# Queries less each head's maximum: two VectorE operations, or two ScalarE multiplications and a GpSimd addition

## The chip, the core and the metric

The kernel runs on one core of one Trainium2 chip. A core has five engines that each work through a queue of instructions in order: TensorE (PE; PEld is its weight load) for matrix products and transpositions, VectorE (DVE), ScalarE (ACT) and GpSimd (POOL) for elementwise work, and SyncE (SP), which issues transfers here. Tiles lie in the on-chip memory SBUF, matmul results in the banks of PSUM. The metric is the device time of one execution in microseconds.

## What is computed

Two decoder layers over x of 16 sequences x 128 tokens x 256 features, each with three blocks. Layer 0 has causal single-head attention, cross attention with 16 heads of 16 features over a context, and a feed-forward network of 16 blocks of 64 of which a router picks four. Layer 1 has self-attention with 16 heads, attention over the context with rotated queries and keys and a mask by position and by cell number, and a mixture of eight experts (two chosen) and two shared ones.

The change lies in the 16-head attention, which three of the six blocks use. For one sequence and each head it is

```python
scores = jnp.einsum('bqhd,bkhd->bhqk', qh, kh) / np.sqrt(D_HEAD)
scores = jnp.where(attention_mask[:, None, :, :], NEG_FILL, scores)
probs = jax.nn.softmax(scores, axis=-1)
out = jnp.einsum('bhqk,bkhd->bqhd', probs, vh)
```

with 1/sqrt(256) and no mask in layer 1's self-attention. A softmax is unchanged when each row's maximum is taken off before the exponential.

## The kernel before, in words

**Order of the work.** The 16 sequences make eight pairs (G = 2). Each pair goes through a layer as a chain of steps written as a Python generator. `Turns` (line 74 on) is a planner that runs while the program is built: it holds up to five such chains at a time, keeps an estimated free time for every engine, and each time resumes the chain that could go on soonest, which then records its next instructions. A step names its engine and the buffers that it takes (`yield DVE, dict(qs=1)`), and `q.give` returns them. The estimates are 150 + 1.05 ns a column for VectorE, 220 + 0.8 for ScalarE, 60 + 1.7 or (two tensors) 60 + 2.5 for GpSimd, and 150 ns for a change of engine. So the order on every engine's queue comes from these estimates, and it is fixed once the program is built. The experts of layer 1 start as further chains when the last pair has left layer 0 and their weights have been asked for (`late_weights`: the two gu loads and down, 3 MB), at most three at a time.

All engines' instructions are recorded by helpers, so that the profile has one line for each: 113 matmuls, 117 transpositions, 121 VectorE, 125 ScalarE, 131 GpSimd. The names of the tiles tell them apart.

**The attention of one sequence** (`attention`, line 471) runs twice over the scores. The 16 heads are two chunks (DC) of eight, and the eight are four rows of 32 features with two heads each (HR). `spread` has made from the keys kT the tile kb, in which, for each of two heads, the other head's features are zeroed and one of them is set to one. The first pass (s<-kb,qT, with the mask added by a product with the identity, s<-ident,unseen) gives the scores with the queries on the partitions; VectorE reduces them to the negative maximum of each query and head (top), which frees the score banks. TensorE transposes top (topT, in a bank). VectorE adds to the queries qT, for each of the two heads, the transposed maxima times a 0/1 column (`heads`) that puts them on the features of the one head's place: this is qs. The second pass (s<-qs,kb) then gives scores less the maximum with the keys on the partitions. Where there is a mask, VectorE adds it (p<-s,unseen); ScalarE takes the exponential; TensorE multiplies with the values (oT), which have a column of ones for the sum, ScalarE copies (oS), TensorE transposes (o), and VectorE divides.

**Buffers** (`LIMITS`, line 332): four general PSUM banks, two score tiles that each pass takes both of (`s=2`), three qs, three top, three tmp. The tmp buffers hold the experts' tanh (sg) and, in the windowed attention, the comparison of cells.

**Around it.** GpSimd computes normalise's reciprocal root in four small operations (rstd, less), spreads the keys (kb, four operations a pair), adds residuals and biases, and rotates queries and keys (qT<-qT,consts, then qT<-qT,swap): the swap tile is made by two DMAs that SP issues, and VectorE multiplies it by the sines between the two. SP's queue holds these, the loads of ctx, of masks and cells, the late weights, and the stores, in one order.

Of the kernel before, what the change touches and what calls it, by code (L numbers as in the profile page):

```python
# [14 lines left out]
ALU = mybir.AluOpType  # L15
AX = mybir.AxisListType

B, S, D = 16, 128, 256
P = 128
DC = D // P  # L20
# [8 lines left out]
HR = RT // HD  # L29
# [41 lines left out]
PE, DVE, ACT, POOL, SP = "PE", "DVE", "ACT", "POOL", "SP"  # L71
# [149 lines left out]
def decoder(ctx: ExitStack, tc: tile.TileContext, a: dict, out: bass.AP):  # L221
# [9 lines left out]
    def bank(shape, name):  # L231
        return ps.tile(shape, F32, tag="bank", name=name)
# [52 lines left out]
    heads = consts[:, C_HEADS : C_HEADS + HR]  # L285
# [8 lines left out]
    def along(t, n):  # L294

        return t.unsqueeze(2).to_broadcast([t.shape[0], t.shape[1], n])
# [30 lines left out]
    for name, scale in (("L0_xattn_bq", 0.25), ("L1_attn_b_q", 0.0625), ("L1_xattn_b_q", 0.25)):  # L327
        t = scaled_bias[name] = keep.tile([P, DC], F32, name=f"scaled_{name}")
# [4 lines left out]
        bank=4, s=2, oT=1, xn=6, xT=5, qk=5, qs=3, kb=4, v=4, p=4, oS=2, on=4, hm=8, tmp=3, rank=2, selT=2, p0=2,  # L333
        pT0=2, unseen=4, cell=2, chosen=3, swap=2, words=2, top=3,
    )
    q = Turns(nc, LIMITS)

    def new(tag, shape, name, dtype=F32):
        return work.tile(shape, dtype, tag=tag, name=name, bufs=LIMITS[tag])
# [127 lines left out]
    def banks():  # L467

        return [ps_s.tile([P, 2, HR, DC, S], F32, tag="s", name="s") for _ in range(2)]

    def attention(qT, kb, v, j, unseen=None, to=None):

        js = slice(j * S, (j + 1) * S)
        yield PE, dict(s=2)
        ss = banks()
        if unseen is not None:  # L480
            for r in range(4):
                q.matmul(
                    ss[r // 2][:, r % 2].rearrange("p h e s -> p (h e) s"), unseen,
                    ident16.unsqueeze(1).to_broadcast([P, HR * DC, S]), start=True, stop=False,
                )
        for e in range(DC):
            for r in range(4):
                at = slice(r * RT, (r + 1) * RT)
                q.matmul(
                    ss[r // 2][:, r % 2, :, e], qT[at, e, js], kb[at, e, :, js],  # L490
                    start=unseen is None, stop=unseen is None or e == DC - 1,
                )
        yield DVE, dict(top=1)
        top = tops.pop(0)
        for t2, s in enumerate(ss):
            q.dve(
                "tensor_reduce", top[:, t2 * 2 * RT : (t2 + 1) * 2 * RT].rearrange("p (h d) -> p h d", d=HD)[:, :, 0:DC],
                s.rearrange("p r h e s -> p (r h) e s"), AX.X, ALU.max, negate=True,
            )
            q.give("s")  # L500
        yield PE, dict(bank=1)
        t = bank([P, S], "topT")
        q.transpose(t, top, ident)
        q.give("top")
        tops.append(top)
        yield DVE, dict(qs=1)
        qs = new("qs", [P, DC, HR, S], "qs")
        for h in range(HR):
            q.dve(
                "scalar_tensor_tensor",  # L510
                qs[:, :, h, :], t.unsqueeze(1).to_broadcast([P, DC, S]), heads[:, h : h + 1], qT[:, :, js],
                ALU.mult, ALU.add,
            )
        q.give("bank")
        yield PE, dict(s=2)
        ss = banks()
        for e in range(DC):
            for h in range(HR):
                for r in range(4):
                    at = slice(r * RT, (r + 1) * RT)  # L520
                    q.matmul(
                        ss[r // 2][:, r % 2, h, e], kb[at, e, h, js], qs[at, e, h, :], start=True, stop=True
                    )
        q.give("qs")

        def exponentials(s):
            s = s.rearrange("p r h e s -> p (r h e) s")
            if unseen is None:
                yield ACT, dict(p=1)
                p = new("p", [P, HC, S], "p")  # L530
                q.act("activation", p, s, AF.Exp)
                q.give("s")
            else:
                yield DVE, dict(p=1)
                p = new("p", [P, HC, S], "p")
                q.dve("tensor_tensor", p, s, unseen.unsqueeze(1).to_broadcast([P, HC, S]), ALU.add)
                q.give("s")
                yield ACT
                q.act("activation", p, p, AF.Exp)
            return p  # L540

        pTs = yield [exponentials(s) for s in ss]
        yield PE, dict(oT=1, bank=1)

        oT = bank([P, H // 4, S], "oT")
        for t2 in range(2):
            for e in range(DC):
                for n in range(2):
                    for i in range(HR):
                        h = e * HC + (2 * t2 + n) * HR + i  # L550
                        c4 = h % 4
                        q.matmul(
                            oT[c4 * CT : (c4 + 1) * CT, h // 4, :],
                            v[:, j, h * HA : h * HA + CT], pTs[t2][:, (n * HR + 1 - i) * DC + e, :],
                            start=True, stop=True,
                        )
        q.give("p", 2)
        yield ACT, dict(oS=1)
        oS = new("oS", [P, H // 4, S], "oS")
        q.act("copy", oS, oT)  # L560
        q.give("oT")
        q.give("bank")
        yield PE, dict(bank=1)
        o = bank([P, H // 4, S], "o")
        for t4 in range(H // 4):
            q.transpose(o[:, t4, :], oS[:, t4, :], ident)
        q.give("oS")
        yield DVE, dict(on=1) if to is None else {}
        o = o.rearrange("p t (c a) -> p (t c) a", a=CT)
        r = small.tile([P, H], F32, tag="r", name="r")  # L570
        q.dve("reciprocal", r, o[:, :, HD])
        if to is None:
            to = new("on", [P, D], "on")
        q.dve("tensor_tensor", to.rearrange("p (h e) -> p h e", e=HD), o[:, :, 0:HD], along(r, HD), ALU.mult)
        q.give("bank")
        return to
# [144 lines left out]
    def context_attention(l):  # L721
# [23 lines left out]
        def one(j):  # L745
            yield POOL, dict(unseen=1)
            unseen = new("unseen", [P, S], "unseen", BF16)
            q.pool("tensor_scalar", unseen, mask[:, j, :], OUT, 1.0, ALU.mult, ALU.mult)
            on = yield from attention(qT, kb, v, j, unseen=unseen)
            q.give("unseen")  # L750
            yield POOL
            q.pool("tensor_tensor", x[l][:, j, :], x[l][:, j, :], on, ALU.add)
            q.give("on")
# [66 lines left out]
    def self_attention(l):  # L820
# [24 lines left out]
        def one(j):  # L845
            on = yield from attention(qT, kb, v, j)
            yield from output_projection(on, w["o1"], l, j, free="on")
# [7 lines left out]
    def windowed_attention(l):  # L855
# [33 lines left out]
        def one(j):  # L889
            b = l * G + j  # L890
            yield DVE, dict(unseen=1, tmp=1)

            other = new("tmp", [P, S], "other")
            q.dve(
                "tensor_scalar",
                other, cell_k[:, j * S : (j + 1) * S], cell_q[:, b : b + 1], -1.0, ALU.is_equal, ALU.add
            )
            unseen = new("unseen", [P, S], "unseen4", BF16)
            q.dve("scalar_tensor_tensor", unseen, other, -OUT, causal_T, ALU.mult, ALU.min)
            q.give("tmp")  # L900
            yield from attention(qT, kb, v, j, unseen=unseen, to=on[:, j, :])
            q.give("unseen")
            yield POOL
            q.pool("tensor_tensor", x[l][:, j, :], x[l][:, j, :], row("L1_xattn_b_o"), ALU.add)
# [230 lines left out]
```

## Time and profile before

| | |
|---|---|
| median of 3 runs (range) | 894.0 us (891.85 to 896.6) |
| the profiled execution | 889.73 us |
| its span, first to last instruction | 887.9 us |
| mean granted TensorE clock | 0.981 |
| instructions | 17836 |
| queries with maxima (qs, VectorE) | 96 operations, 451 to 485 ns |
| maxima (top, VectorE) | 96 operations, 1191 to 1225 ns |
| first and last attention's maxima start at | 53.6 and 725.2 us |

The profile shows one execution. The busy time of an engine is the time in which it executes something. A wait is put down to the instruction that ended last before the waiting one started. The chain of waits goes back from the last instruction, at each step to what released it. A group line names output and inputs, shape and count, and then busy time and the mean duration of one; the figure behind the bar is the engine's idle time in front of these instructions. In the chain, pieces of one kind that follow each other are merged, and their count stands behind the x.

### The profile page before, as it was taken

How to read it: one execution, taken by the hardware profiler on the slowest of the kernel's cores; microseconds unless marked ns; L12 is line 12 of the kernel's file. 1: busy time of each engine (PE TensorE's matmuls, PEld its weight loads, DVE VectorE, ACT ScalarE, POOL GpSimd, SP SyncE). 2: the span in 40 equal slices, each digit the busy share in tenths (PEclk: the TensorE clock that was granted, in tenths of full speed). 3: DMA queues.
4: the chain of work that ended last, by engine and by line, in shares of the span. 5: the costliest groups of instructions: out<-in, count | busy, mean ns of one | idle time of the engine just before them, and what ended most of it. 6: DMA issues, size and time to landing. Idle time of an engine off the chain costs nothing.

```text
span 887.9 us, 17836 instructions
## 1 busy us (share of the span) xinstructions
PE 834.6 (94%) x7232; PEld 671.9 (76%) x7232; DVE 578.5 (65%) x1378; ACT 348.0 (39%) x705; POOL 286.7 (32%) x558
## 2 busy tenths in 40 slices
PE   3999999999999999999798989979998999999998
PEld 2867778778777777877666857758786878888887
DVE  4358866456458476278588969676887686556443
ACT  2435443453435253444534625434633323122111
POOL 4023534124334225273762742405251402000000
PEclk9999999999999999999998989989997999999999
DMA  9400000000000000231000100101010000000000
GB/s 341 154 3 15 3 1 13 2 16 13 3 1 14 1 2 1 70 116 44 18 25 1 43 1 1 43 18 38 13 32 13 30 1 13 13 1 13 12 13 13
DMA packets 16961, 25.94 MB, mean 29 GB/s; under 512 B 3184, under 2 KB 12400, under 8 KB 16240
## 3 DMA queue, kind: packets, MB, share of 16 engines
q1 hardware_dynamic: 16880, 24.81, 8.2%
q8 instruction: 57, 0.93, 0.4%
q14 instruction: 24, 0.20, 0.1%
HBM read 18.51 MB, written 2.10 MB: 23 GB/s over the span
## 4 chain that ended last, share of the span: by engine, by line
PE 78%; DVE 11%; POOL 5%; ACT 3%; DMA 2%; issue 2%; SPq 0%; POOLq 0%; ACTq 0%; DVEq 0%
PE gu L113 15%; PE y L113 14%; PE s L113 12%; PE pj L113 9%; PE pr L113 7%; PE hp L113 7%; PE oT L113 4%; PE tps L117 2%; DVE top L121 2%; PE o L117 2%; DVE st L121 1%; POOL rstd L131 1%; PE rt L113 1%; DVE qs L121 1%; POOL kb L131 1%
## 5 line engine op out<-in xcount | busy, mean ns | idle before, releaser
L121 DVE TENSOR_REDUCE top<-s 128x8 f32<-128x1024 f32 x96 | 112.7, 1216 | 30.7 <-PE s L113 30.4
L113 PE MATMUL gu<-srcT,gu 128*128 128x256 f32 x512 | 117.7, 381 | 0.7 <-ACT oT L125 0.3
L113 PEld LDWEIGHTS gu<-srcT,gu 128*128 128x128 f32 x512 | 94.7, 190 | 14.6 <-ACT oT L125 0.6
L131 POOL TENSOR_SCALAR rstd<-mv 128x2 f32<-128x2 f32 x72 | 16.8, 233 | 236.1 <-DVE mv L121 203.2
L121 DVE TENSOR_TENSOR p<-s,unseen 128x1024 f32<-128x1024 f32 x64 | 76.0, 1217 | 21.0 <-PE s L113 21.0
L125 ACT ACTIVATE sg<-gu 128x256 f32<-128x256 f32 x80 | 30.6, 383 | 135.8 <-PE gu L113 134.3
L125 ACT ACTIVATE p<-p 128x1024 f32<-128x1024 f32 x64 | 66.8, 1059 | 35.8 <-DVE p L121 35.3
L113 PE MATMUL s<-qs,kb 32*128 32x128 f32 x1536 | 61.8, 293 | 8.6 <-DVE top L121 7.3
L113 PEld LDWEIGHTS s<-qs,kb 32*128 32x128 f32 x1536 | 51.4, 194 | 22.2 <-issue 10.7
L113 PE MATMUL hp<-srcT,L_w 128*128 128x256 f32 x256 | 66.0, 387 | 0.0
L131 POOL TENSOR_TENSOR eq<-eq,consts 128x512 f32<-128x512 f32 (+1 forms) x16 | 14.7, 916 | 157.2 <-DVE eq L121 157.2
L113 PE MATMUL y<-L_w,hm 128*128 128x256 f32 x256 | 58.9, 383 | 0.0
L113 PE MATMUL y<-down,hm 128*128 128x256 f32 x256 | 58.6, 382 | 0.0
L113 PE MATMUL s<-kb,qT 32*128 32x256 f32 x768 | 56.5, 406 | 0.0
L131 POOL TENSOR_SCALAR kb<-kT,consts 128x256 f32<-128x256 f32 x96 | 52.7, 562 | 11.7 <-ACT kT L125 10.9
L121 DVE TENSOR_TENSOR x<-x,y 128x256 f32<-128x256 f32 x32 | 13.4, 420 | 64.9 <-PE y L113 64.9
L113 PEld LDWEIGHTS hp<-srcT,L_w 128*128 128x128 f32 x256 | 44.3, 190 | 12.3 <-issue 2.4
L131 POOL TENSOR_TENSOR rstd<-rstd,power 128x2 f32<-128x2 f32 x72 | 51.7, 717 | 6.0
L121 DVE SCALAR_TENSOR_TENSOR sg<-sg,gu 128x256 f32<-128x256 f32 x80 | 33.3, 416 | 31.2 <-ACT sg L125 31.1
L113 PEld LDWEIGHTS y<-L_w,hm 128*128 128x128 f32 x256 | 47.6, 190 | 7.9 <-issue 1.1
L113 PE MATMUL oT<-p,v 128*32 128x128 f32 x1536 | 52.8, 277 | 0.4 <-ACT p L125 0.3
L113 PEld LDWEIGHTS y<-down,hm 128*128 128x128 f32 x256 | 47.7, 190 | 6.8 <-DVE hm L121 0.4
(150 smaller groups left out, 1671.7 us busy)
## 6 DMA issues: line engine op xcount, KB each, us to landing
c<-in_ctx SPq DMA_DIRECT2D x16, 256.0 KB, 2.9
x<-in_x SPq DMA_DIRECT2D x8, 256.0 KB, 6.0
L_w<-in_L_w SPq DMA_DIRECT2D x2, 1024.0 KB, 8.6
swap<-qT SPq DMA_DIRECT2D x16, 128.0 KB, 2.0
swap<-kT SPq DMA_DIRECT2D x16, 128.0 KB, 2.1
gu<-in_L_gu SPq DMA_DIRECT2D x2, 1024.0 KB, 5.0
out_x<-x SPq DMA_DIRECT2D x8, 256.0 KB, 2.1
down<-in_L_down SPq DMA_DIRECT2D x1, 1024.0 KB, 7.0
```

The source lines that it names most:

```text
L113: self.nc.tensor.matmul(out, lhsT, rhs, **kw)
L117: self.nc.tensor.transpose(out, src, ident)
L121: getattr(self.nc.vector, name)(out, *args, **kw)
L125: getattr(self.nc.scalar, name)(out, *args, **kw)
L131: getattr(self.nc.gpsimd, name)(out, *args, **kw)
```

## The change

The two VectorE operations become three of other engines. ScalarE multiplies the transposed maxima by each of the two 0/1 columns into a new tile `less` of 128x256, which is taken from the tmp buffers, and then returns the bank. GpSimd adds `less`, repeated over the two chunks, to the queries, repeated over the two heads, in one operation of 512 columns.[...]

```diff
         q.transpose(t, top, ident)
         q.give("top")
         tops.append(top)
-        yield DVE, dict(qs=1)
+        yield ACT, dict(tmp=1)
+        less = new("tmp", [P, HR, S], "less")
+        for h in range(HR):
+            q.act("mul", less[:, h, :], t, heads[:, h : h + 1])
+        q.give("bank")
+        yield POOL, dict(qs=1)
         qs = new("qs", [P, DC, HR, S], "qs")
-        for h in range(HR):
-            q.dve(
-                "scalar_tensor_tensor",
-                qs[:, :, h, :], t.unsqueeze(1).to_broadcast([P, DC, S]), heads[:, h : h + 1], qT[:, :, js],
-                ALU.mult, ALU.add,
-            )
-        q.give("bank")
+        shape = [P, DC, HR, S]
+        q.pool(
+            "tensor_tensor", qs, qT[:, :, js].unsqueeze(2).to_broadcast(shape), less.unsqueeze(1).to_broadcast(shape), ALU.add
+        )
+        q.give("tmp")
         yield PE, dict(s=2)
```

No other line differs, but the planner works with the new steps and their estimates, so the order of nearly everything after the first attention is another one, on every queue.

## Prediction

> **What bounds the kernel now.** I read the page first, then a table of the span in stretches, the waits, the chain of waits in time, and the instruction orders of both built kernels.
>
> The page: busy times, and the chain that ended last by engine and by line.
>
> ```profile
> PE 834.6 (94%) x7232; PEld 671.9 (76%) x7232; DVE 578.5 (65%) x1378; ACT 348.0 (39%) x705; POOL 286.7 (32%) x558
> ...
> PE 78%; DVE 11%; POOL 5%; ACT 3%; DMA 2%; issue 2%; SPq 0%; POOLq 0%; ACTq 0%; DVEq 0%
> PE gu L113 15%; PE y L113 14%; PE s L113 12%; PE pj L113 9%; PE pr L113 7%; PE hp L113 7%; PE oT L113 4%; PE tps L117 2%; DVE top L121 2%; PE o L117 2%; DVE st L121 1%; POOL rstd L131 1%; PE rt L113 1%; DVE qs L121 1%; POOL kb L131 1%
> ```
>
> TensorE is the bound, and the change takes no work from it. Only TensorE's idle time, 887.9 - 834.6 = 53.3 us, and what the others do to it, can move.
>
> The stretches (columns: stretch, length, then busy us of PE, PEld, DVE, ACT, POOL, then the granted clock):
>
> ```profile
> 0.00:60.00 60.00, 44.55 (x247) 36.59 (x247) 23.83 (x78) 22.56 (x58) 18.08 (x52) 1.00 0.52 184
> 60.00:120.00 60.00, 56.81 (x636) 44.31 (x636) 48.26 (x104) 28.96 (x58) 22.98 (x45) 1.00 0.03 7
> 440.00:540.00 100.00, 89.30 (x983) 68.38 (x981) 82.00 (x187) 45.65 (x85) 50.19 (x93) 0.93 0.06 20
> 540.00:640.00 100.00, 93.54 (x1009) 73.37 (x1005) 75.37 (x162) 47.67 (x88) 31.45 (x61) 0.97 0.07 25
> 740.00:888.00 148.00, 143.97 (x740) 124.30 (x732) 78.67 (x240) 26.71 (x70) 10.32 (x26) 1.00 0.03 11
> ```
>
> 60 - 44.6 = 15.4 us of the idle time is the start, and 4.0 us the last stretch, in which no attention runs. The other 34 us lie between 60 and 740 us, where all 48 attentions are. Where TensorE idles most (440 to 540), VectorE is 82% busy and the clock is below 1.
>
> The waits between 60 and 740 us (sum us, times, longest):
>
> ```profile
> PE s L113 <- DVE top L121: 7.3, 5, 3.2
> PE topT L117 <- DVE qs L121: 6.0, 3, 3.1
> ...
> PE tps L117 <- DVE qs L121: 2.5, 1, 2.5
> ```
>
> The groups by shape (count, busy us, mean ns):
>
> ```profile
> L121 DVE SCALAR_TENSOR_TENSOR qs<-topT,consts,qT 128x256 f32<-128x256 f32 x96 | 41.7, 476 | 14.7 <-PE topT L117 13.7 <-PE s L113 0.7
> ...
> L131 POOL TENSOR_TENSOR eq<-eq,consts 128x512 f32<-128x512 f32 x8 | 11.4, 1422 | 63.2 <-DVE eq L121 63.2
> ...
> L131 POOL TENSOR_TENSOR kT<-kT,consts 128x512 f32<-128x512 f32 x8 | 10.2, 1269 | 0.0
> ...
> L125 ACT COPY pT<-pt 128x128 f32<-128x128 f32 x16 | 3.9, 274 | 10.9 <-PE pt L117 10.8
> ```
>
> The chain through the longest stall (start, us):
>
> ```profile
> 466.28 0.78 DVE qs L121 x2
> 467.07 2.26 DVE top L121 x2
> ...
> 472.53 0.76 DVE qs L121 x2
> 473.29 2.27 DVE top L121 x2
> 475.57 0.14 issue
> 475.70 2.08 PE s L113 x28
> ```
>
> Here the queries stand in VectorE's queue ahead of the maxima (top) that free the score banks; TensorE waits for the maxima, not for the queries.
>
> **What the Trainium skill says.** "Perfetto Trace Analysis", Identifying the Most-Contended Engine: matmul busy time flatters TensorE, weight-load busy time is the better measure. It agrees: weight loads are busy 124.3 of 148 us (84%) in the last stretch but 68% from 440 to 540. "ScalarE: Activation LUTs", What ACT_TABLE_LOAD costs: 186 ns + 0.833 ns a column, and some 93 ns for each pointer operand. The trace agrees on the pointer: the 128x256 copies out of PSUM (oT, v) take 375 ns, the biased hm 471. "GPSIMD Engine Reference", 3.1: a two-input operation costs about 2.6 cycles an element at 1.2 GHz, by estimate 1.1 us for 512; the trace's 1.27 to 1.42 us decide. "SBUF — State Buffer", Who interferes with whom: a VectorE instruction with two SBUF inputs and a GpSimd instruction that reads SBUF lock each other out; one with a single SBUF input does not. The trace fits: the 512-column swap product, two SBUF inputs, has a minimum of 672 ns, a mean of 888 and a maximum of 1646, while top and p, which read PSUM, keep to 1191 to 1226.
>
> **The change part by part.** Removed: 96 VectorE operations, 41.7 us. On the chain the pair appears eleven times, summed piece by piece 8.9 us (the page's 1%), nearly always as something in front of another operation. In two of these (578.7 and 674.5 us) TensorE waits right behind the pair; ScalarE then stands there for 0.74 us instead, so they gain almost nothing, and at 402.6 the maximum is late next anyway. That leaves 8.9 - 0.77 - 0.79 - 0.79 = 6.6 us; I take -6.6, between 0 and -8.9 for the pieces alone. The bound of a full relief is higher: of TensorE's waits 7.3 + 6.0 + 2.5 us name top and qs, and unseen, p and v another 5.8, together 21.6 us.
>
> Added on ScalarE: 96 multiplications of 128x128 out of PSUM with a pointer scale. The plain copy takes 274 ns, the pointer 471 - 375 = 96: 370 ns, 35.5 us in all. By the skill's figures it is 186 + 107 + 93 = 386. ScalarE goes from 348 to 384 us (43%); behind the multiplication in its queue stand exponentials (1.06 us), which feed TensorE's oT, but ScalarE idles over half of every stretch after 60 us. Cost nothing; if that cover fails, 0.74 us at a place.
>
> Added on GpSimd: 48 additions of 512 columns. Nearest rows 1269 and 1422 ns: I take 1.35 us, 65 us in all, GpSimd from 287 to 352 us. Both operands are broadcast over four dimensions, which no row shows; if each took twice that, 2.7 us, it would be 130.
>
> Latency: a pair took 0.95 us from the transposition (2 x 476 ns); now 0.74 + 1.35 us and one more hop between engines (some 0.1 us a hop on the chain): 2.3 us, with waiting room 2.6. I took from the two built orders how much TensorE work stands between each topT and its score matmuls, each matmul at the trace's spacing (0.43 us for 128x256, 1.17 for 16 of s<-qs, 1.08 for 16 of oT). Before, one of 48 lies under 1.35 us and the shortage sums to 1.1 us; after, four lie under 2.6 us, shortage 3.5. Cost +2.4; ends 0 and +9 (the sum at 3.5 us, 8.7).
>
> GpSimd's queue: the addition stands behind everything there. Three kinds of instruction matter: the rotation, whose first product waits for the swap DMA (12.5 and 19.0 us were its two waits before, harmless then); the spreading of keys, four of 0.56 us behind ScalarE's kT; and normalise's four, 1.4 us. In the stretches 414 to 427 and 500 to 515 us GpSimd alone carries the chain, 27 us. Attentions come at 6 in 80 and 9 in 100 us there, 0.08 a us, so 2.2 additions of 1.35 us fall into these stretches: +3.0; ends 0 and +10, the upper end where one addition is held behind a late swap for the 7.2 us that the ctx load took behind the late weights at 383 us. In the changed order SP issues the two gu and the down load ahead of the first query swap instead of behind it; that swap then shares the DMA queue with 3 MB. Its GpSimd product has one key addition in front and six instructions before the next query addition, whose scores come 6 us after their transposition: I put it at nothing, 5 us if the cover is gone.
>
> The order: the builder picks the next step by its estimated costs, so all queues move. The score banks are taken by every score pass and are freed some 2.6 us after it (two maxima or two sums of 1.22 us and hops). Summed over the orders, the TensorE work between one pass and the next falls short of 2.6 us by 16.9 us before and 21.5 after: +4.6; ends -5 and +12. The worst cluster before (6.2 us short) is the 460 to 480 us stall, where PE idled 5.8, so the measure has some hold. After, the worst is 8.5 and a second one has 5.8. The first expert matmul, the filler, has 2603 matmuls in front of it instead of 2505; the attention's end moves little (412 instead of 434 left behind it).
>
> The clock: from 420 to 700 us it was below 1 in eight 20 us slices, worth 17 us, in or just behind the slices with idle time; 17 / 34 is half a us for each us of idle. Sum: -6.6 + 2.4 + 3.0 + 4.6 = +3.4, times 1.5 = **+5.1 us**. The profiled execution, span 887.9, took 889.7 us in all: 894.8. It ran 4.3 us below the median of the runs, so on the median **899.1**.
>
> **Rivals.** *VectorE's relief decides* (the other side): of the 21.6 us of waits on VectorE between 60 and 740 us a third goes, 7.2 us, as VectorE falls from some 80% to 74% busy in the crowded stretches, and clock with it, x1.5: -10.8, so 883. It decides from the point where the new additions find GpSimd free, so that the latency and queue terms (5.4 us) vanish. For it: in the long stalls the chain is solid VectorE. Against: the orders show more crowding of the score banks. *Covered*: relief and new waits cancel, 894, for TensorE is full in half the slices. *GpSimd becomes the bound*: additions at 2.7 us, or held behind rotations; another 48 x 1.35 = 65 us on GpSimd, of which a quarter shows, 16: 915. *It doesn't do what it says* is excluded: in the built order VectorE has 96 operations less, ScalarE 96 and GpSimd 48 more.
>
> **How the numbers follow.** A change under 0.5% (4.5 us) can't be told from none here. Slightly slower, my forecast: 0.38, 899, own range 896 to 907. GpSimd the bound: 0.12. Covered: 0.17. Relief: 0.33. Of the forecast's 0.38 some 0.06 lie within the bound, and 0.02 of the covered case lie above it: slower 0.46, same 0.21, faster 0.33. The range leaves out half of the GpSimd case and the lower third of the relief case: 880 to 912.
>
> **What would show it.** VectorE's busy time down by about 42 us, ScalarE's up by 34 to 37, GpSimd's by 61 to 68. qs additions at 1.3 to 1.45 us. TensorE's waits naming GpSimd's qs in sum 3 to 10 us, and POOL above 5% on the chain. Idle time between 60 and 740 us at 36 to 40 instead of 34 us. Wrong if that idle time falls under 30 us, or if the additions take over 2 us.

## Result: faster by 0.9%

| | kernel before | kernel after |
|---|---|---|
| median (range), 6 runs each | 893.36 us (890.36 to 896.6) | 884.63 us (883.16 to 887.65) |
| ratio, 95% interval | | 0.9907 (0.9879 to 0.9936) |
| the profiled execution | 889.73 us | 883.19 us |
| its span | 887.9 us | 881.4 us |
| mean granted clock | 0.981 | 0.988 |

The gain is clear of noise, 8.3 us by the ratio. The forecast was 899, slower. The time lies within the stated range of 880 to 912, but on the other side of the kernel before, 1.6 us above the 883 of the rival "VectorE's relief decides".

### The profile after

The page of the kernel after: busy times, then the chain that ended last by engine and by line.

```profile
PE 833.8 (95%) x7232; PEld 669.4 (76%) x7232; DVE 546.8 (62%) x1282; ACT 376.4 (43%) x801; POOL 346.4 (39%) x606
...
PE 80%; DVE 8%; POOL 6%; ACT 3%; issue 2%; DMA 1%; SPq 0%; POOLq 0%; DVEq 0%; ACTq 0%
PE gu L113 15%; PE y L113 14%; PE s L113 13%; PE pj L113 10%; PE pr L113 8%; PE hp L113 7%; PE oT L113 5%; PE tps L117 2%; PE o L117 2%; DVE p L121 2%; DVE top L121 1%; POOL rstd L131 1%; POOL kb L131 1%; PE rt L113 1%; DVE st L121 1%
```

TensorE's work is the same and its idle time falls from 53.3 to 881.4 - 833.8 = 47.6 us. VectorE's share of the chain falls from 11 to 8%, qs leaves the list, and GpSimd gains only one point.

Stretches of the span (stretch, length, then busy us of PE, PEld, DVE, ACT, POOL, then the clock). The one with all the attentions, in the kernel before:

```profile
60.00:740.00 680.00, 646.08 (x6253) 510.96 (x6257) 475.98 (x1062) 298.74 (x577) 258.32 (x480) 0.97 0.06 19
```

And in the kernel after, with the start, the crowded stretch and the end:

```profile
0.00:60.00 60.00, 44.57 (x246) 36.91 (x247) 23.21 (x77) 23.27 (x60) 16.02 (x49) 1.00 0.53 189
60.00:740.00 680.00, 652.31 (x6286) 514.40 (x6285) 450.37 (x983) 327.88 (x676) 323.55 (x540) 0.98 0.06 19
...
440.00:540.00 100.00, 93.51 (x1022) 70.86 (x1021) 82.58 (x185) 56.56 (x113) 68.17 (x120) 0.95 0.07 20
...
740.00:882.00 142.00, 136.96 (x704) 118.04 (x702) 73.19 (x224) 25.24 (x66) 6.80 (x18) 1.00 0.03 10
```

The start idles 15.4 us, as before, and the end 4.4 (881.4 - 740 - 137.0) instead of 3.9. The gain lies between: 680 us less the busy time leave 27.7 us of idle time from 60 to 740 us instead of 33.9. VectorE is still 83% busy from 440 to 540, but with another 4 us of TensorE's work done there.

The waits of TensorE from 60 to 740 us, the longest six (sum us, times, longest):

```profile
PE tps L117 <- DVE xn L121: 3.8, 3, 2.4
PE o L117 <- ACT oS L125: 3.3, 5, 0.8
PE s L113 <- DVE p L121: 2.2, 3, 1.0
PE pj L113 <- ACT srcT L125: 2.1, 5, 0.7
PE s L113 <- DVE top L121: 2.0, 4, 0.8
PE s L113 <- ACT p L125: 1.9, 3, 0.9
```

All waits that name VectorE sum to 13.6 us instead of 21.6, those on ScalarE to 12.7 instead of 11.9. None of them names GpSimd's qs. The addition shows only in the waits of the weight loads, which stand in TensorE's queue with the score products: there it is named at four places, 2.5 us in sum and 1.8 at the longest.

The new operations, by shape (count, busy us, mean ns):

```profile
L131 POOL TENSOR_TENSOR qs<-qT,less 128x512 f32<-128x512 f32 x48 | 61.6, 1283 | 129.1 <-ACT less L125 128.8
L125 ACT ACTIVATE less<-topT,consts 128x128 f32<-128x128 f32 x96 | 30.1, 367 | 59.3 <-PE topT L117 59.2
```

In front of 29 of the 48 additions GpSimd sits idle, 128.8 us in sum, until ScalarE's product is there: in this order it has room there, and it waits for its input.

The chain through the longest wait of a score product for a sum of VectorE's (p) in the kernel after, 1.0 us at 460.4 us (start, us):

```profile
452.37 2.33 DVE top L121 x2
454.69 0.60 DVE swap L121
455.29 0.33 DVE x L121
455.62 2.27 DVE top L121 x2
...
460.17 1.23 DVE p L121
461.40 0.04 issue
461.44 2.08 PE s L113 x28
```

It is the same kind of stall as the one that the prediction shows, made of VectorE's maxima and sums on the way to free score banks, without the two pairs of qs that stood among them. Before, such a wait was up to 3.2 us long.

### The profile page after: what moved, and what is told of

It reads as the page before. It is cut to its first block, busy times and chain, and to the rows that moved or that the text cites. A ratio compares the mean times of both kernels' runs of the same rounds, so it can differ in the third digit from the quotient of the medians.

```text
span 881.4 us, 17923 instructions
## 1 busy us (share of the span) xinstructions
PE 833.8 (95%) x7232; PEld 669.4 (76%) x7232; DVE 546.8 (62%) x1282; ACT 376.4 (43%) x801; POOL 346.4 (39%) x606
## 4 chain that ended last, share of the span: by engine, by line
PE 80%; DVE 8%; POOL 6%; ACT 3%; issue 2%; DMA 1%; SPq 0%; POOLq 0%; DVEq 0%; ACTq 0%
PE gu L113 15%; PE y L113 14%; PE s L113 13%; PE pj L113 10%; PE pr L113 8%; PE hp L113 7%; PE oT L113 5%; PE tps L117 2%; PE o L117 2%; DVE p L121 2%; DVE top L121 1%; POOL rstd L131 1%; POOL kb L131 1%; PE rt L113 1%; DVE st L121 1%
## 5 line engine op out<-in xcount | busy, mean ns | idle before, releaser
L131 POOL TENSOR_TENSOR qs<-qT,less 128x512 f32<-128x512 f32 x48 | 61.6, 1283 | 129.1 <-ACT less L125 128.8
L113 PEld LDWEIGHTS gu<-srcT,gu 128*128 128x128 f32 x512 | 94.5, 190 | 13.6 <-DVE x L121 0.5
L121 DVE TENSOR_TENSOR p<-s,unseen 128x1024 f32<-128x1024 f32 x64 | 75.4, 1216 | 26.6 <-PE s L113 26.4
L125 ACT ACTIVATE less<-topT,consts 128x128 f32<-128x128 f32 x96 | 30.1, 367 | 59.3 <-PE topT L117 59.2
L117 PE MATMUL tps<-consts,xn 128*128 128x128 f32 x224 | 35.9, 288 | 19.4 <-DVE xn L121 18.2
```

Source lines behind the costliest of these rows:

```text
L113: self.nc.tensor.matmul(out, lhsT, rhs, **kw)
L117: self.nc.tensor.transpose(out, src, ident)
L121: getattr(self.nc.vector, name)(out, *args, **kw)
L125: getattr(self.nc.scalar, name)(out, *args, **kw)
L131: getattr(self.nc.gpsimd, name)(out, *args, **kw)
```

## Experiments

The change does two things at once: other engines do the work, and the planner, which knows it, makes another order for every queue. The runs take the two apart. Ratios are to the kernel before; 0.0010 is 0.9 us. The kernel after has 0.9907 (0.9879 to 0.9936).

| operations of the step | order made for the two VectorE operations | order made for ScalarE and GpSimd |
|---|---|---|
| two on VectorE | 1 (kernel before) | 1.0058 (1.0036 to 1.0079) |
| two on ScalarE, one on GpSimd | 1.0108 (1.0086 to 1.0129) | 0.9907 (kernel after) |
| none | 0.9891 (0.9859 to 0.9924) | 0.9884 (0.9860 to 0.9907) |

### The new operations in the old order

In the kernel before (this and the diffs below are shortened):

```diff
         for h in range(HR):
-            q.dve("scalar_tensor_tensor", qs[:, :, h, :], ...)
+            q.charge(DVE, 150 + 1.05 * DC * S)
+            nc.scalar.mul(less[:, h, :], t, heads[:, h : h + 1])
+        nc.gpsimd.tensor_tensor(qs, ...)
```

`charge` tells the planner of the two VectorE operations, so TensorE's order is that of the kernel before; ScalarE and GpSimd get theirs at the same places. `less` has one buffer.

> The order that the planner made for the kernel before on every engine, but the two VectorE operations are replaced by the two ScalarE multiplications and the GpSimd addition at the same places; the product has one buffer of its own. Theory R (relief: VectorE's queue is shorter by 41.7 us, whatever the order): VectorE's waits shrink here too, 893.4 falls by 5 to 9 us, to 884 to 888. Theory O (the new order is what gains): no gain here, 892 to 900, as the longer way through two queues meets an order that left only 1.35 us for it. My forecast's terms (latency +2.4, GpSimd's queue +3.0, relief -6.6) give 892, within 3.

902.4 us, ratio 1.0108 (1.0086 to 1.0129). Both theories and my terms are missed: it is slower by 1%. The waits of TensorE in this run, 60 to 740 us:

```profile
PE s L113 <- POOL qs L513: 11.2, 6, 3.3
PE o L117 <- ACT oS L125: 4.7, 4, 2.8
PE s L113 <- DVE unseen L121: 3.7, 1, 3.7
PE topT L117 <- DVE top L121: 3.3, 2, 2.3
```

Here is the wait that I had feared, 11.2 us at six places, where the score matmuls follow the transposition too closely. So the latency is real, but what it costs depends on the order.

The same with `less` in the shared tmp buffers:

> As the run before it, with the product in the three tmp buffers that the experts use too, without the planner knowing of it. Theory R: the same as that run within 3 us. If buffers matter, it differs from it by more, slower where experts and attention mix (520 to 740 us).

900.4 us, ratio 1.0088 (1.0067 to 1.0109): within 3 us of its twin. The buffer isn't the reason.

### The old operations in the new order

In the kernel after, the planner is charged for ScalarE and GpSimd, and the two VectorE operations are recorded at the addition's place; TensorE's order is that of the kernel after.

```diff
         yield POOL, dict(qs=1)
-        q.pool("tensor_tensor", qs, ...)
+        q.charge(POOL, 60 + 2.5 * DC * HR * S)
+        for h in range(HR):
+            nc.vector.scalar_tensor_tensor(qs[:, :, h, :], ...)
```

> The order that the planner made for the changed kernel, TensorE's identical, but the queries are made by the two VectorE operations, put into VectorE's queue where the addition was recorded. Theory R: VectorE is as loaded as before, so the gain goes, 892 to 900. Theory O: the gain stays, 883 to 887.

897.9 us, ratio 1.0058 (1.0036 to 1.0079): theory R's number, against theory O. The new order isn't better in itself; with the old operations in it, it loses to the old order.

### The load put back on VectorE, nothing else

```diff
+        for h in range(HR):
+            nc.vector.tensor_scalar(spare, qT[:, :, js], heads[:, h : h + 1], None, ALU.mult)
         q.give("tmp")
```

> The changed kernel with the load put back on VectorE and nothing else: two operations of 128x256 (the queries times a column, some 0.41 us each, 39 us in all) into a spare tile that nobody reads, where the addition is recorded. Theory R: the gain goes, 891 to 898. Theory O: it stays within 3 us of the changed kernel's 884.6. If only the earlier return of the PSUM bank gains, it stays too.

905.9 us, ratio 1.0146 (1.0122 to 1.0170), 21 us above the kernel after (0.0239 x 892), more than either theory said. The bank is returned early here too, so its earlier return doesn't make the gain. VectorE's busy time rose by 51.9 us, not 39, and nobody waits for the result: a load of which the planner doesn't know costs 0.4 us for each us of it. The page of this run, busy times:

```profile
PE 844.9 (94%) x7232; PEld 676.0 (75%) x7232; DVE 598.7 (66%) x1378; ACT 376.9 (42%) x801; POOL 348.8 (39%) x606
```

About half of the 21 us is idle time of TensorE (903.1 - 844.9 = 58.2 us instead of 47.6); from 60 to 740 us its waits that name VectorE sum to 21.3 us instead of 13.6. The other half stands in its busy time, up by 11.1 us with the same work. The mean clock is 0.981 instead of 0.988, but the kernel before has 0.981 as well and a busy time of 834.6, so the clock doesn't explain it; the cause of this half stays open.

### The step left out, in both orders

The second pass takes the queries themselves (no maximum is taken off), and the exponentials get a scale of 0.01. The planner is still charged for the step, so each order stays.

```diff
-            ..., kb[at, e, h, js], qs[at, e, h, :], start=True, stop=True
+            ..., kb[at, e, h, js], qT[at, e, js], start=True, stop=True
```

> The kernel before in its own order on TensorE, with the step left out altogether: no operation makes qs, the second pass takes the queries themselves, so nothing is taken off, and the exponentials have a scale of 0.01 so that they stay finite. It shows what relief alone is worth in the old order, without new waits and without GpSimd's and ScalarE's work: theory R 878 to 886; my forecast's own term (-6.6, with clock -10) 883; theory O (VectorE's load matters little, only the order) 890 to 894.

> The changed kernel in its own order on TensorE, with the step left out: no product, no addition, the second pass takes the queries themselves, the exponentials have a scale of 0.01. What the changed kernel takes above this is what the new operations still cost by waits and queues in the order made for them. My forecast put +5.4 us and clock on it, so 876 to 878 here; if the planner hides them whole, 883 to 886.

884.2 and 881.5 us. The first is theory R's; the second lies between my forecast's 876 to 878 and the 883 to 886 of costs that are hidden whole. The stretch from 60 to 740 us, busy us of PE, PEld, DVE, ACT, POOL, first in the old order:

```profile
60.00:740.00 680.00, 653.12 (x6312) 515.88 (x6311) 447.19 (x986) 300.43 (x582) 262.64 (x490) 0.98 0.06 20
```

then in the new one:

```profile
60.00:740.00 680.00, 656.24 (x6331) 519.58 (x6330) 447.13 (x996) 301.12 (x584) 261.29 (x488) 0.98 0.06 19
```

The first number is what relief alone is worth, the pair's time on the way to the scores included: 0.0109, 9.7 us. Against it the second (0.9884) says that the orders themselves, without the step, differ by 0.0007, less than the intervals can tell. And against the kernel after it says what the new operations still cost in the order made for them: 0.0023, 2 us, also within the intervals. In the old order they cost 1.0108 - 0.9891 = 0.0217, 19 us. The VectorE pair depends on the order too: it costs 9.7 us in its own and 1.0058 - 0.9884 = 0.0174, 15.5 us, in the other.

### The addition made twice

> The changed kernel in its own order with every GpSimd addition made twice, one after the other: 61.6 us more on GpSimd and 1.28 us more on the way of every attention's queries, of which the planner knows nothing. If GpSimd's queue or the latency is near to being late in this order, each us shows at perhaps a third of the 48 places, +15 to +25 us over the changed kernel, 900 to 910. If both are well covered (theory R, in which only VectorE's queue counts), +0 to +6, 885 to 891.

```diff
         q.pool("tensor_tensor", qs, ...)
+        nc.gpsimd.tensor_tensor(qs, ...)
         q.give("tmp")
```

901.7 us, ratio 1.0086 (1.0054 to 1.0118): 16 us above the kernel after, at the lower end of the first expectation. The longest wait of TensorE in this run, 60 to 740 us:

```profile
PE s L113 <- POOL qs L517: 12.3, 11, 2.6
```

The second addition is as long as the first and costs 16 us, where the whole new step cost about 2; the planner doesn't know of it. VectorE's busy time rose as well, from 546.8 to 558.2 us with the same operations (the swap product from 839 to 986 ns in the mean), so not all of the 16 us need be the wait for qs. GpSimd's time isn't free; the planner's order had covered the first addition, and not much more.

### The lottery of orders

`HOP`, the planner's estimate for a change of engine, at 100 and 200 instead of 150 ns: every operation stays, the order changes.

> The kernel before, with the planner's estimate of a change of engine at 100 ns instead of 150; no operation differs, only the order. It measures the lottery of orders: if it is as large as the change's gain (theory L: the gain is luck of the order), this lies anywhere from 880 to 910; if it is small, within 5 us of 892.

> The kernel before with that estimate at 200 ns. As for 100 ns: theory L 880 to 910, else within 5 us of 892.

> The changed kernel with the planner's estimate of a change of engine at 100 ns. If the gain belongs to the operations given an order made for them, it is 5 to 12 us faster than its twin of the kernel before at 100 ns. If it is luck of the order (theory L), the two can lie either way.

> The changed kernel with that estimate at 200 ns, to be held against its twin at 200 ns: 5 to 12 us faster if the gain is systematic, either way if it is luck of the order.

| HOP | kernel before | kernel after | difference of the ratios |
|---|---|---|---|
| 100 | 1.0005 (0.9986 to 1.0023) | 0.9952 (0.9935 to 0.9969) | -0.0053 |
| 150 | 1 | 0.9907 (0.9879 to 0.9936) | -0.0093 |
| 200 | 1.0069 (1.0042 to 1.0096) | 0.9939 (0.9918 to 0.9961) | -0.0130 |

All three pairs are faster, by 5, 8 and 12 us (the first 4.7, just under the forecast's lower end), and in none do the two intervals touch. At 200 the kernel before moves by 6 us, more than the 5 expected of a small lottery. The order alone moves either kernel by up to 4 to 6 us, so the sign is the operations' and the size is in part the order's.

### The same move once more

```diff
         def one(j):
-            if j:
+            if True:
                 yield ACT
                 q.act("activation", xn[:, j, :], ...)
```

> The changed kernel, and normalise's last step of the first sequence of each pair too is made by ScalarE (0.60 us) instead of VectorE (0.43 us, 72 operations, some 30 us): the same kind of move once more, known to the planner. If VectorE's load is what costs between 60 and 740 us, another 3 to 8 us faster than the changed kernel, 877 to 882; if VectorE is no longer late, or two operations in a row on ScalarE delay the chains' beginnings, 884 to 890.

880.0 us, ratio 0.9867 (0.9845 to 0.9889): 3.6 us faster than the kernel after by the ratios, though the two intervals overlap; it is the fastest version with the whole computation. VectorE has lost another 26.4 us of busy time (520.4 instead of 546.8). But where the profiled execution (882.4 us, the slowest of the six) gains is not where VectorE's load was thought to cost:

```profile
0.00:60.00 60.00, 48.74 (x280) 39.12 (x281) 23.75 (x76) 27.94 (x67) 21.02 (x59) 1.00 0.52 184
60.00:740.00 680.00, 651.38 (x6300) 515.20 (x6301) 428.30 (x934) 359.18 (x747) 319.24 (x533) 0.99 0.06 20
```

In the first 60 us TensorE idles 11.3 us instead of 15.4: its first transposition starts at 9.4 us instead of 14.5, because ScalarE makes the first half of the normalised tile at once, which in the kernel after (at 14.0 us) stood in VectorE's queue behind the statistics of a pair whose load was still on its way. From 60 to 740 us TensorE idles 28.6 us, where the kernel after has 27.7. The waits that name VectorE fall there from 13.6 to 10.2 us, and now a wait for the addition is the largest:

```profile
PE s L113 <- POOL qs L131: 6.0, 5, 1.9
```

So the forecast's number was met by another mechanism, and this run doesn't show that a further relief of VectorE pays.

## Why the prediction was wrong

The step that failed is the sum of new costs, +10.0 us for latency, GpSimd's queue and the order, laid over a relief of 6.6. About 2 us were measured for all three. The largest of them, the order's +4.6, turned the sign: without it the sum is -1.2.

**What bounds the kernel: right.** The profiled execution is shorter by 6.5 us. TensorE's idle time between 60 and 740 us falls by 6.2, the end idles 0.5 more, and TensorE's busy time falls by 0.8. The sign "wrong if that idle time falls under 30 us" came true, with 27.7.

**The relief, -6.6 us and half again for the clock, -9.9: right in size, in part by luck.** Leaving the step out of the old order measured -9.7, and 7.0 us of it is idle time between 60 and 740 us. But the chain before has thirteen pairs of qs and not eleven (those at 77.6 and 646.4 us were missed), 10.6 us instead of 8.9, so that the same reckoning would have given -8.2, and the factor for the clock isn't shown (below).

**The prices: right.** 367 ns for the product (370), 1283 for the addition (1350); the double price for the fourfold broadcast is refuted. ScalarE's busy time rose by 28.4 us and GpSimd's by 59.7, a little under the stated 34 to 37 and 61 to 68.

**Latency, +2.4 us: wrong.** No wait of a matmul names qs, and the weight loads' waits for it are 2.5 us at four places, which count for latency and queue together. I counted the shortage between topT and s<-qs as if TensorE were on time at each; that where the addition comes late other waits are already there is my reading, not shown.

**GpSimd's queue, +3.0 us: wrong.** I took the stretches of the old execution in which GpSimd carried the chain and laid the additions on top of them (the chain shows 32 us of it, from 414.4 to 427.4 and from 496.5 to 515.9, not 27). But the planner moves the other work as well, and GpSimd's busy time counts against room that it has: it waits 129 us for products. This step and the latency together are the 2 us between the kernel after and its order without the step, which the intervals can't tell from nothing.

**The order, +4.6 us: wrong, and this turned the sign.** The shortage of score banks rose from 16.9 to 21.5 us by my count, and without the step the two orders are alike (0.9891 and 0.9884). TensorE's waits for score banks (on top, and on p of VectorE and ScalarE) are 6.1 us after; before, top and p of VectorE made 8.6. The count had hit the one stall that I tested it on and proved nothing for the others: it takes VectorE as free at once, and where its queue is full the gap says little (argued, not tried). Nor does it see other stalls: the longest single wait before was not in that stall (3.2 us) but 3.7 us for a mask (unseen) at 519.3 us. Waits of this kind sum to 3.8 us before and 3.9 in the old order without the step, and to 0.6 in the new order with and without it.

The measured 2 us in place of the 10 give -9.9 + 2 = -7.9, near the measured -8.3; the agreement leans on the lucky size of the relief. The rival of the other side had the mechanism in its words, "from the point where the new additions find GpSimd free". VectorE's busy time fell by 31.7 us, not by 42: part is given back in longer operations, and part is that less of it overlaps.

**The clock's half us for each us: not shown.** The slices below full clock between 60 and 740 us were worth 17.0 us before and 10.4 after, for 33.9 and 27.7 us of idle time. But the two don't go together elsewhere. In the old order without the step idle time falls by 7.0 us and these slices only from 17.0 to 15.4; with the new operations in the old order it rises by 9.4 and they from 17.0 to 17.2. And TensorE's busy time, in which slower products would have to stand, is 834.6 us before and 833.8 after.

## What to carry to other kernels

Moving work off the engine that the bound waits for can pay even when the new way is longer and goes through two queues, if whatever sets the order knows of the new way: here 8.3 us for 41.7 us taken from VectorE, a fifth. The same operations in an order made for the old ones lost 1%. So an added latency is to be priced in the order made for it, by what waits there, and not by laying it over the old execution. Where an order is made by a planner, one comparison holds its luck as well: shift one estimate and compare twins before believing a size. And a forecast that is met is no proof of its mechanism: the last move (normalise on ScalarE) gained in the first 60 us, by what stood in front of one tile in a queue.

## What the runs showed of the hardware beside this

VectorE's scaling of 128x256 (xn) has one SBUF tensor as input and takes 407 to 412 ns at the median in both kernels; single ones are stretched beside GpSimd. In the kernel before one kind of it, xn<-xn, kept to 402 to 414 ns, and the others reached 599 to 758; after, the maxima of the four kinds are 1178 to 1360. The timeline of VectorE in the kernel after:

```profile
433.11 1.02 DVE L121 TENSOR_SCALAR xn<-c,mv,rstd 128x256 f32<-128x256 f32 x1
434.06 1.35 DVE L121 TENSOR_SCALAR xn<-xn,mv,rstd 128x256 f32<-128x256 f32 x1
```

and of GpSimd:

```profile
432.71 1.27 POOL L131 TENSOR_TENSOR qT<-qT,swap 128x512 f32<-128x512 f32 x1 [0.69 <-DVE swap L121]
433.94 1.32 POOL L131 TENSOR_TENSOR kT<-kT,consts 128x512 f32<-128x512 f32 x1
```

Each scaling ends about 0.15 us after the GpSimd operation beside it (434.13 after 433.98, 435.41 after 435.26). The Trainium skill, "SBUF — State Buffer", Who interferes with whom, counts tensor_scalar among the operations that can take the ports shared with GpSimd, although it has a single SBUF input; the timeline fits that, though no run shows the ports themselves. All xn together rose by 6.0 us (2.7 + 1.3 + 1.3 + 0.7) from the kernel before to the one after; in the new order without the additions two of these groups rose by 2.5 (0.9 + 1.6), so it isn't all the additions' doing (the GpSimd operations shown here are of the rotation). In the run with the load put back, the spare operation, of the same class, took 354 ns at the median and 1861 at most.
